# A recurrent kernel on one core: in four late steps, the order of the candidate seed and of the update gate's activations is that of the steps before them, and two steps place one filling unit elsewhere

## The chip, the cores and the metric

The kernel runs on one core of a Trainium2 chip. The metric is the device time of one execution in microseconds (us); the time of a kernel is the median of several runs. Engines are called as the profile calls them: PE (TensorE matmuls), PEld (its weight loads), DVE (VectorE), ACT (ScalarE), POOL (GpSimd), SP (SyncE, which issues most DMAs).

## What is computed

A gated recurrent unit runs over 128 steps for 64 sequences of width 512, in float32, and its outputs are added to its inputs. Every fourth step but the last passes the state through one more matrix (a "prop" step).

```python
def step(h, inp):
    x_t, prop = inp
    comb = jnp.concatenate([x_t, h], axis=-1)
    z = jax.nn.sigmoid(comb @ Wz + bz)
    r = jax.nn.sigmoid(comb @ Wr + br)
    comb2 = jnp.concatenate([x_t, r * h], axis=-1)
    h_cand = jnp.tanh(comb2 @ Wh + bh)
    h_new = (1.0 - z) * h + z * h_cand
    h_next = jnp.where(prop, jnp.tanh(h_new @ Wp + bp), h_new)
    return (h_next, h_new)
...
x = x + _L0_cond_ref(x, cond_1024, ...)     # h0 is cond_1024; prop in steps 3, 7, ... 123
```

## The kernel before

**Two halves.** The 64 sequences are split in two halves of 32, called half 0 and half 1 (`h` in the code). Each half is a Python generator, `half(h)`, that emits the instructions of its steps and yields the columns of each piece of PE work; a loop at the end always advances the half that has emitted fewer columns, half 1 starting 700 columns behind. That sets the order of the instructions in every engine's queue. A matmul of half h uses two of the four 32-column groups of the PE array, so the matmuls of both halves run beside each other, but they are issued in one order: where the first one in the queue waits, the others wait behind it.

**One step.** For each half: the gate matmuls R (line 1076), the sigmoid of r, `rh` = r·h, its transpose `rhT` (lines 1080-1082); the gate matmuls Z (line 1092); `places[0]` filling units (line 1127); the candidate's matmuls H (line 1129), which need `rhT`; the tanh `c` (line 1134); c·z, `h` = c·z - keep, and its transpose `hT` (lines 1136-1139); `places[1]` filling units (line 1149). R of the next step needs `hT`. In a prop step the gate P follows (line 1151), its tanh `hprop`, its transpose, and `places[2]` units. Below, R0, Z0, H0, P0 are the gates of half 0 and R1, Z1, H1, P1 those of half 1, with the step in brackets: R0(122).

**Filling units.** The input's share of the gates (x times the upper half of the weights) doesn't depend on the state. It is cut in units of PE work that stand in a queue; `fill(n, h)` takes the next n. The table `PLACES` (by step modulo 8) and the table `TAIL` (for the last steps, T = 128) say how many units a step places before H, after H, and after P. For the steps up to 125 the shares are computed for four steps together by a scheme with fewer multiplications (units of 192 columns); ACT, DVE and POOL combine their results into `cp`, from which each step's share `G[t]` is read. The shares of steps 126 and 127 (`wide_step`) are made straight in PSUM by `wide_unit` (four matmuls of 128 columns a half).

**Seeds.** `seed(i, t, h)` (line 439) is an ACT copy that writes a step's share of gate i from `cp` into the PSUM bank on which the gate's matmuls then add up: `rec` for R and H of each half, `rec_z` for Z of both halves. It appears in the profile as ACT COPY at L442.

**Late steps.** `late(t)` (line 834) holds for steps 121 (T - 7) and 123, 124, 125 (and the wide steps, where no seeds are made). In other steps, called body steps here, the seed of H for step t + 1 is emitted behind the tanh of step t (line 1145), or behind the prop's transpose (line 1159). In a late step it is emitted inside the step, behind the transpose of `rh` (line 1084). In a body step, half 1 emits the sigmoids of z of both halves behind its gate Z (`gate_z(slice(0, S), range(S))`, line 1115): four ACT instructions into PSUM (`rec_z`), and one DVE instruction of 256 columns for `keep` = (z - 1)·h. In a late step, half 1 emits there only those of half 0 (line 1113); those of half 1 come behind its gate H, just ahead of its tanh (line 1133); they go to a tile `z` in SBUF (line 1096), and `keep` is made by two DVE instructions of 128 columns.

Step 121 takes the last six 192-column units; behind it, POOL makes `G[124]` and `G[125]` from them (line 911). Steps 122 to 125 take units of the wide steps. Step 123 is a prop step.

Of the kernel before, what the change touches and what calls it, by code (L numbers as in the profile page):

```python
# [9 lines left out]
F32 = mybir.dt.float32  # L10
# [8 lines left out]
def kernel(  # L19
# [15 lines left out]
    B, T, D = x.shape  # L35
    H = h0.shape[1]
    P = 128
    S = 2
    V = B // S
    NQ = P // V  # L40
    J = H // NQ
# [6 lines left out]
    R, Z, H_ = range(3)  # L48
# [10 lines left out]
    one = ctx.enter_context(tc.tile_pool(name="one", bufs=1))  # L59
# [128 lines left out]
    z = rec[2][:, 1]  # L188

    def gate_ps(i, h):  # L190
        return rec[2][:, 0] if i == Z else rec[h][:, 0 if i == R else 1]
# [63 lines left out]
    def gate(i, h, lT, w):  # L255
        for k in range(K):
            products(gate_ps(i, h), h, lT[:, h, ts(k, V)], lambda c: quarters(w)[:, c, k])
            yield S * J
# [17 lines left out]
    def crossed(dst, h, i, func, ordered=True):  # L276
        for d in range(2):
            o, v = dst[ts(d, 2 * V)], gate_ps(i, h)[ts(h, 2 * V), d, :]
            if ordered:
                o, v = state_order(o), plain_order(v)  # L280
            nc.scalar.activation(o, v, func)  # L281

    def turn(dst, src):
        nc.vector.transpose(out=dst, in_=src)
# [154 lines left out]
    def seed(i, t, h):  # L439
        if t < T - WIDE:  # L440
            rows = slice(None) if i == Z else ts(h, 2 * V)
            nc.scalar.copy(  # L442
                gate_ps(i, h)[rows].rearrange("p d (c n) -> p d c n", c=C),
                G[t][rows, :, :, i, :].rearrange("p c d n -> p d c n"),
            )
# [308 lines left out]
    def pair_right(a, p1, x_, g=1):  # L754
# [6 lines left out]
    )  # L761
    HEAD = {0: (4, 6, 0), 1: (8, 6, 0), 2: (16, 12, 0), 3: (8, 6, 8), 4: (6, 8, 0)}
    TAIL = {
        T - 10: (6, 8, 0), T - 9: (1, 7, 5), T - 8: (1, 7, 0), T - 7: (0, 6, 0), T - 6: (1, 5, 0),
        T - 5: (0, 5, 3), T - 4: (1, 5, 0), T - 3: (2, 0, 0),
    }

    WIDE = 2
# [61 lines left out]
    both(8)  # L830

    state = {0: (h_init, hT)}

    def late(t):
        return t == T - 7 or t >= T - 5

    made = {}
    kept_h = {}
# [1 line left out]
    def shared(t, name, new):  # L840
        if (t, name) not in made:
            made[t, name] = new()
        return made[t, name]

    def new_two(name, t):
        return shared(t, name, lambda: two.tile([P, S, J], F32, tag=name, name=f"{name}_{t}"))

    def new_first(t):
        return shared(t, "h", lambda: one.tile([P, S, J], F32, tag=f"h{t}", name=f"h_{t}"))

    def new_turned(tag, name, t):
        return shared(t, name, lambda: new_T(tag, f"{name}_{t}"))

    def begin(t):
        u = (t - 3) % 8
        even = FIRST + 2 * ((t - 3) // 8)
        if t == 1:
            put(batch((1, 0), [(1, 1), (1, 2)]))
        elif t == 2:
            put(batch((1, 1), [(1, 10), (1, 11)]) + batch((1, 2), [(1, 8), (1, 9)]))  # L860
        elif t == 3:
            put(batches(FIRST))
        elif u == 7:
            put(batches(even + 2))
        if t == T - 10:
            put(
                batch((LAST, 0), [(LAST - 1, 4), (LAST, 1)])
                + batch((LAST, 1), [(LAST, 2), (LAST, 10)])
                + [wide_unit(T - 2, i, k) for i in (R, Z, H_) for k in range(K)]
                + [wide_bias(T - 2), crossing_unit()]  # L870
                + [wide_unit(T - 1, i, k) for i in (R, H_, Z) for k in range(K)]
                + [wide_bias(T - 1)]
            )

    def behind_r(t, duo, u):
        odd = FIRST + 2 * duo + 1
        if t == 2:
            pair_left(0, 1, 2)
            sum_inner(7, nc.gpsimd)
        elif t == 3:  # L880
            pair_right(0, 1, 10)
        if t == 4:
            sum_inner(4, nc.gpsimd)
        if u == 0 and duo >= 1 and odd - 2 < LAST:
            outer_u2(odd - 2)
# [171 lines left out]
    def half(h):  # L1057

        for t in range(T):
            g, j = divmod(t, Q4)  # L1060
            prop = j == CHUNK - 1 and t < T - 1
            last = t == T - 1
            duo, u = divmod(t - 3, 8)
            places = HEAD.get(t) or TAIL.get(t) or PLACES[u]
            if h == 0:
                begin(t)
            if t >= T - WIDE:
                yield from wide_step(t, h)
                if last:
                    return  # L1070
                if h == 1:
                    behind_step(t, duo, u, state[t + 1][0])
                continue
            h_old, hT = state[t]

            yield from gate(R, h, hT, wh[R])
            if h == 1:
                behind_r(t, duo, u)
            rh, rhT = new_two("rh", t), new_turned("rhT", "rhT", t)
            crossed(r_, h, R, AF.Sigmoid)  # L1080
            nc.vector.tensor_mul(rh[:, h, :], r_, h_old[:, h, :])  # L1081
            turn(rhT[:, h, :], rh[:, h, :])
            if late(t) or t == 0:
                seed(H_, t, h)
            if t not in (3, T - 5):
                seed(R, t + 1, h)
            if h == 1:
                join(t, duo, u, 0)

            if t == 0:  # L1090
                yield from fill(2 * K - 2, h)
            yield from gate(Z, h, hT, wh[Z])
            keep = new_two("keep", t)
            z_ = z
            if late(t):
                z_ = shared(t, "z", lambda: one.tile([P, S, J], F32, tag="o12", name=f"z_{t}"))

            def gate_z(part, halves, h_old=h_old, z_=z_, keep=keep):
                for i in halves:
                    crossed(z_[:, i, :], i, Z, AF.Sigmoid)  # L1100
                kept = keep[:, part, :], z_[:, part, :], h_old[:, part, :]
                nc.vector.scalar_tensor_tensor(  # L1102
                    out=kept[0],
                    in0=kept[1],
                    scalar=1.0,
                    in1=kept[2],
                    op0=ALU.subtract,
                    op1=ALU.mult,
                )

            if h == 1:
                if late(t):
                    gate_z(0, (0,))
                else:
                    gate_z(slice(0, S), range(S))
                join(t, duo, u, 1)
                if t == 1:
                    sum_raw34(1)
                    sum_inner(6, nc.gpsimd)
                if t == 0:  # L1120
                    join_x(1, 0)
                    join_x(1, 1)
                    sum_raw12(1)
                if t == 2:
                    for n in range(2, 4):
                        join_x(2, n)
            yield from fill(places[0], h)

            yield from gate(H_, h, rhT, wh[H_])
            h_new = new_two("h", t) if t > 1 else new_first(t)  # L1130
            cand = new_two("c", t)
            if late(t) and h == 1:
                gate_z(1, (1,))
            crossed(cand[:, h, :], h, H_, AF.Tanh)
            c = z_[:, h, :]
            nc.vector.tensor_mul(c, cand[:, h, :], c)
            hT = new_turned("hT", "hT", t)
            nc.vector.tensor_sub(h_new[:, h, :], c, keep[:, h, :])  # L1138
            turn(hT[:, h, :], h_new[:, h, :])
            if t == T - WIDE - 1:  # L1140
                made_by[t + 1, None, h] = at[h] + 820
            if prop:
                nc.scalar.copy(gate_ps(P_, h)[ts(h, 2 * V)], bias_p[ts(h, 2 * V)])
            elif not late(t + 1):
                seed(H_, t + 1, h)
            if h == 1:
                seed(Z, t + 1, 0)
            state[t + 1] = h_new, hT
            yield from fill(places[1], h)
            if prop:  # L1150
                yield from gate(P_, h, hT, wp)
                h_next = new_two("hprop", t)
                hT = new_turned("hT", "hpT", t)
                crossed(h_next[:, h, :], h, P_, AF.Tanh)
                turn(hT[:, h, :], h_next[:, h, :])
                if t in (3, T - 5):
                    seed(R, t + 1, h)
                if not late(t + 1):
                    seed(H_, t + 1, h)
                state[t + 1] = h_next, hT  # L1160
                yield from fill(places[2], h)
            if h == 1:
                behind_step(t, duo, u, h_new)
# [6 lines left out]
    while any(live):  # L1170
        h = 0 if live[0] and (not live[1] or at[0] <= at[1]) else 1
# [46 lines left out]
```

## Time and profile before

| | us |
|---|---|
| three runs | 1254.91, 1256.15, 1256.37; median 1256.15 |
| the profiled execution's own time | 1255.74 |
| its span, from the first to the last instruction of the program | 1253.6 |
| PE busy | 1246.9 (99% of the span) |
| PEld busy | 1174.0 (94%) |
| DVE, ACT, POOL busy | 806.2, 830.0, 908.8 |
| granted clock of PE | 1.0 |

The profile is one execution, 2.1 us of which lie outside the span. Times in its timelines count from the span's start. A row of the timeline view has the start, the time from the start of the first to the end of the last of some equal instructions in a row, the engine, the line, the operation, the tile written <- the tiles read, their shapes and number, and in brackets how long the engine was idle before them and whose work ended the wait. The releaser is inferred from what ended last before, and can be another.

### The profile page before, as it was taken

What the parts mean: (1) busy time and instruction counts of PE and PEld (TensorE: products, weight loads), DVE (VectorE), ACT (ScalarE), POOL (GpSimd) and SP (SyncE); (2) the same over time, 40 slices, a digit from 0 to 9 for tenths busy, and PEclk for the clock granted to TensorE, in tenths of its full rate; (3) what the DMA queues carried; (4) which work ended last, traced back from release to release, by engine and by line L of the source; (5) the groups of instructions that cost most, each with busy time, mean ns of one, the idle gap of its engine ahead of it and who ended that gap; (6) DMA issues with size and microseconds to landing.
All of it is one profiled execution on the core that took longest, in us unless ns stands there. A gap on an engine that the chain in (4) does not pass through costs nothing.

```text
span 1253.6 us, 61573 instructions
## 1 busy us (share of the span) xinstructions
PE 1246.9 (99%) x26384; PEld 1174.0 (94%) x26384; DVE 806.2 (64%) x2177; ACT 830.0 (66%) x2666; POOL 908.8 (72%) x1032
## 2 busy tenths in 40 slices
PE   9999999999999999999999999999999999999998
PEld 5899999999999999999999999999999999999987
DVE  5666666666666666666666666666666666666554
ACT  2566666766666676766666667666666666666664
POOL 4988777777876778767778677786777777777630
PEclk9999999999999999999999999999999999999999
DMA  8311212121111110221201211111111112111011
GB/s 257 83 31 42 53 37 53 36 54 39 35 53 49 41 49 24 53 53 37 54 24 49 53 41 50 36 43 47 53 38 39 49 39 53 39 52 27 12 39 35
DMA packets 112360, 61.14 MB, mean 49 GB/s; under 512 B 12844, under 2 KB 109368, under 8 KB 112088
## 3 DMA queue, kind: packets, MB, share of 16 engines
q1 hardware_dynamic: 111656, 56.90, 16.8%
q8 instruction: 208, 3.41, 1.2%
q14 instruction: 64, 0.52, 0.1%
q0 software_dynamic: 256, 0.14, 0.1%
q10 hardware_dynamic: 176, 0.16, 0.0%
HBM read 40.38 MB, written 16.78 MB: 46 GB/s over the span
## 4 chain that ended last, share of the span: by engine, by line
PE 99%; DMA 1%; SPq 0%; DVE 0%; issue 0%; ACT 0%
PE rec L246 44%; PE rec_z L246 16%; PE scratch_r L246 14%; PE scratch_q L246 11%; PE scratch_a L246 5%; PE scratch_y L246 4%; PE scratch_x L246 4%; DMA wx<-in_L_cond_Wr_dram 1%; PE scratch_a L541 0%; PE scratch_r L541 0%; PE scratch_q L541 0%; PE scratch_y L541 0%; PE scratch_x L541 0%; SPq L127 0%; SPq L141 0%
## 5 line engine op out<-in xcount | busy, mean ns | idle before, releaser
L246 PE MATMUL rec<-wh,rhT 128*32 128x256 f32 x4032 | 370.1, 379 | 0.0
L246 PE MATMUL rec<-wh,hT 128*32 128x256 f32 x3008 | 276.2, 379 | 0.0
L246 PE MATMUL rec_z<-wh,hT 128*32 128x256 f32 x3008 | 276.2, 379 | 0.0
L246 PEld LDWEIGHTS rec<-wh,rhT 128*32 128x32 f32 x4032 | 247.5, 110 | 16.7 <-ACT rec L442 0.3
L281 ACT ACTIVATE scratch_r<-rec 64x128 f32<-64x128 f32 x504 | 126.0, 250 | 129.9 <-PE rec L246 65.4
L442 ACT COPY rec<-cp 64x256 f32<-64x256 f32 x504 | 186.9, 371 | 19.4 <-DVE cp L483 0.2
L246 PEld LDWEIGHTS rec_z<-wh,hT 128*32 128x32 f32 x3008 | 190.5, 110 | 6.2
L246 PEld LDWEIGHTS rec<-wh,hT 128*32 128x32 f32 x3008 | 184.0, 110 | 11.2 <-ACT rec_z L442 0.4
L281 ACT ACTIVATE rec_z<-rec_z 64x128 f32<-64x128 f32 x488 | 122.0, 250 | 91.3 <-PE rec_z L246 79.7
L281 ACT ACTIVATE c<-rec 64x128 f32<-64x128 f32 x504 | 136.7, 271 | 61.5 <-PE rec L246 50.4
L968 POOL TENSOR_TENSOR xr<-xr,h 128x256 f32<-128x256 f32 x125 | 109.3, 874 | 85.8 <-DVE h L1138 71.9
L711 POOL TENSOR_TENSOR cp<-mb,mb 128x768 f32<-128x768 f32 x76 | 139.1, 1830 | 9.4 <-DVE mb L677 5.7
L711 POOL TENSOR_TENSOR mb<-mb,mb 128x768 f32<-128x768 f32 x58 | 106.3, 1832 | 45.8 <-DVE mb L677 45.8
L711 POOL TENSOR_TENSOR cp<-mb 128x768 f32<-128x768 f32 x46 | 84.3, 1832 | 56.8 <-ACT rec_z L442 55.4
L246 PE MATMUL scratch_r<-tw,s 128*32 128x192 f32 x928 | 120.9, 326 | 0.0
L650 ACT COPY cq<-scratch_q 128x384 f32<-128x384 f32 x212 | 102.1, 481 | 19.4 <-PE scratch_q L246 17.9
L667 DVE TENSOR_TENSOR cx<-scratch_r,cx 128x384 f32<-128x384 f32 x106 | 59.0, 557 | 84.5 <-PE scratch_r L246 69.0
L246 PE MATMUL scratch_q<-tt,s 128*32 128x192 f32 x928 | 103.6, 326 | 0.0
L1102 DVE SCALAR_TENSOR_TENSOR keep<-rec_z,h 128x256 f32<-128x256 f32 x91 | 38.6, 424 | 95.6 <-ACT rec_z L281 89.2
L673 DVE TENSOR_TENSOR mb<-scratch_q,cx 128x384 f32<-128x384 f32 x106 | 59.0, 557 | 62.5 <-ACT cq L650 62.5
L1081 DVE TENSOR_TENSOR rh<-scratch_r,h 128x128 f32<-128x128 f32 x188 | 54.8, 292 | 59.2 <-ACT scratch_r L281 59.2
L246 PE MATMUL rec<-wp,hT 128*32 128x256 f32 x992 | 91.4, 379 | 0.0
(250 smaller groups left out, 3899.9 us busy)
## 6 DMA issues: line engine op xcount, KB each, us to landing
out_dram<-xr SPq DMA_DIRECT2D x250, 64.0 KB, 1.8
xr<-in_x_dram SPq DMA_DIRECT2D x248, 64.0 KB, 2.1
xs<-in_x_dram SPq DMA_DIRECT2D x240, 64.0 KB, 2.1
wx<-in_L_cond_Wz_dram SPq DMA_DIRECT2D x2, 512.0 KB
wx<-in_L_cond_Wh_dram SPq DMA_DIRECT2D x2, 512.0 KB, 9.5
wh<-in_L_cond_Wr_dram SPq DMA_DIRECT2D x2, 512.0 KB
wh<-in_L_cond_Wz_dram SPq DMA_DIRECT2D x2, 512.0 KB, 5.5
wh<-in_L_cond_Wh_dram SPq DMA_DIRECT2D x2, 512.0 KB
```

The source lines that it names most:

```text
L246: nc.tensor.matmul(ps[part(2 * h + c)], lhsT=left, rhs=rhs(c), start=start, stop=True, skip_group_check=True,)
L281: nc.scalar.activation(o, v, func)
L442: nc.scalar.copy(gate_ps(i, h)[rows].rearrange("p d (c n) -> p d c n", c=C), G[t][rows, :, :, i, :].rearrange("p c d n -> p d c n"),)
L650: nc.scalar.copy(c[:, :nm], ps[:, :nm])
L667: nc.vector.tensor_add(T2[what][:, :nm], r_ps[:, :nm], T2[what][:, :nm])
L673: nc.vector.tensor_add(blocks(1, 1), runs(q_ps[:, :nm]), runs(T2[what][:, :nm]))
L711: nc.gpsimd.tensor_add(dst, a, b)
L968: nc.gpsimd.tensor_add(o, o, h_new.rearrange("p h (k e) -> p h e k", k=K))
L1081: nc.vector.tensor_mul(rh[:, h, :], r_, h_old[:, h, :])
L1102: nc.vector.scalar_tensor_tensor(out=kept[0], in0=kept[1], scalar=1.0, in1=kept[2], op0=ALU.subtract, op1=ALU.mult,)
```

## The change

In four steps (121, 123, 124, 125), the H seed moves from inside the step to the end of the step before; the four sigmoids of z come together behind gate Z and write `rec_z`; `keep` is one DVE instruction. The function `late` is gone. In steps 121 and 123, one unit per half moves from behind gate H to ahead of it. The number of matmuls, of weight loads, of ACT instructions and of DMAs is as before; DVE has four instructions fewer.

```diff
     TAIL = {
-        T - 10: (6, 8, 0), T - 9: (1, 7, 5), T - 8: (1, 7, 0), T - 7: (0, 6, 0), T - 6: (1, 5, 0),
-        T - 5: (0, 5, 3), T - 4: (1, 5, 0), T - 3: (2, 0, 0),
+        T - 10: (6, 8, 0), T - 9: (1, 7, 5), T - 8: (1, 7, 0), T - 7: (1, 5, 0), T - 6: (1, 5, 0),
+        T - 5: (1, 4, 3), T - 4: (1, 5, 0), T - 3: (2, 0, 0),
     }
...
-    def late(t):
-        return t == T - 7 or t >= T - 5
-
...
             turn(rhT[:, h, :], rh[:, h, :])
-            if late(t) or t == 0:
+            if t == 0:
                 seed(H_, t, h)
...
             z_ = z
-            if late(t):
-                z_ = shared(t, "z", lambda: one.tile([P, S, J], F32, tag="o12", name=f"z_{t}"))
...
             if h == 1:
-                if late(t):
-                    gate_z(0, (0,))
-                else:
-                    gate_z(slice(0, S), range(S))
+                gate_z(slice(0, S), range(S))
...
-            if late(t) and h == 1:
-                gate_z(1, (1,))
             crossed(cand[:, h, :], h, H_, AF.Tanh)
...
-            elif not late(t + 1):
+            else:
                 seed(H_, t + 1, h)
...
                 if t in (3, T - 5):
                     seed(R, t + 1, h)
-                if not late(t + 1):
-                    seed(H_, t + 1, h)
+                seed(H_, t + 1, h)
```

## The prediction

> **What bounds the kernel now.** The page first, then the span by steps, then the weight loads, ACT and DVE around the four late steps. The page names one engine for the whole span:
>
> ```profile
> PE 1246.9 (99%) x26384; PEld 1174.0 (94%) x26384; DVE 806.2 (64%) x2177; ACT 830.0 (66%) x2666; POOL 908.8 (72%) x1032
> PE 99%; DMA 1%; SPq 0%; DVE 0%; issue 0%; ACT 0%
> ```
>
> PE has the same matmuls after the change, so all that can move is the time in which PE waits, and only from the end of step 120 on. The windows below are steps 120 to 125, each from its first sigmoid of r to the next one's. Columns: busy time and instructions of PE, PEld, DVE, ACT, POOL, then clock and DMA.
>
> ```profile
> 1190.56:1198.34 7.78, 7.78 (x167) 7.38 (x163) 4.33 (x13) 4.68 (x17) 0.96 (x2) 1.00 0.29 71
> 1198.34:1206.41 8.07, 8.07 (x159) 6.19 (x155) 4.63 (x15) 6.24 (x20) 0.00 (x0) 1.00 0.25 69
> 1206.41:1213.63 7.22, 7.22 (x187) 6.79 (x183) 3.80 (x12) 4.21 (x15) 6.55 (x4) 1.00 0.01 2
> 1213.63:1224.27 10.64, 10.64 (x270) 9.82 (x266) 4.15 (x14) 7.20 (x24) 3.25 (x4) 1.00 0.07 16
> 1224.27:1232.07 7.80, 7.80 (x197) 6.84 (x192) 3.47 (x12) 5.03 (x17) 0.87 (x1) 1.00 0.23 56
> 1232.07:1239.73 7.66, 7.66 (x229) 7.03 (x224) 3.47 (x12) 3.91 (x14) 0.67 (x1) 1.00 0.01 2
> ```
>
> PE busy hides its waits here (8.07 of 8.07): the end of a matmul is modelled. Weight loads show them. Between 1198 and 1239 us only three groups of loads have idle time ahead of them:
>
> ```profile
> 1201.14 0.36 PEld L246 LDWEIGHTS rec<-wh,rhT 128*32 128x32 f32 x10 [0.30 <-ACT rec L442]
> ...
> 1203.38 0.28 PEld L246 LDWEIGHTS scratch_q<-tt,s12r 128*32 128x32 f32 x4
> 1203.59 0.17 PEld L246 LDWEIGHTS rec<-wh,hT 128*32 128x32 f32 x4
> ...
> 1205.07 0.39 PEld L246 LDWEIGHTS rec<-wh,hT 128*32 128x32 f32 x10 [0.44 <-ACT rec_z L442]
> ...
> 1220.39 0.39 PEld L246 LDWEIGHTS rec<-wp,hT 128*32 128x32 f32 x10 [0.20 <-issue]
> ```
>
> The first is H1(121), the second R1(122), the third P1(123): 0.30 + 0.44 + 0.20 = 0.94 us. **That is all there is to win.** R0(122) at 1203.59 follows its half's last unit without a gap: half 0 has no idle time there, and none to spare.
>
> ACT and DVE in step 121, which is late, then ACT and DVE in step 122, whose order is the body's:
>
> ```profile
> 1198.90 0.83 ACT L442 COPY rec<-cp 64x256 f32<-64x256 f32 x2
> 1199.75 0.54 ACT L281 ACTIVATE scratch_r<-rec 64x128 f32<-64x128 f32 x2
> 1200.31 0.77 ACT L442 COPY rec<-cp 64x256 f32<-64x256 f32 x2
> 1201.11 0.55 ACT L281 ACTIVATE z<-rec_z 64x128 f32<-64x128 f32 x2
> 1201.85 0.55 ACT L281 ACTIVATE c<-rec 64x128 f32<-64x128 f32 x2 [0.18 <-PE rec L246]
> 1203.40 0.56 ACT L281 ACTIVATE c<-rec 64x128 f32<-64x128 f32 x2
> 1204.39 0.38 ACT L442 COPY rec_z<-cp 128x256 f32<-128x256 f32 x1
> 1206.41 0.53 ACT L281 ACTIVATE scratch_r<-rec 64x128 f32<-64x128 f32 x2 [1.15 <-DVE mb L676]
> ...
> 1200.64 0.31 DVE L284 STREAM_TRANSPOSE rhT<-rh 128x128 f32<-128x128 f32 x1
> 1203.16 0.31 DVE L284 STREAM_TRANSPOSE hT<-h 128x128 f32<-128x128 f32 x1
> 1204.64 0.31 DVE L284 STREAM_TRANSPOSE hT<-h 128x128 f32<-128x128 f32 x1
> ```
>
> ```profile
> 1208.79 1.09 ACT L281 ACTIVATE rec_z<-rec_z 64x128 f32<-64x128 f32 x4 [0.48 <-PE rec_z L246]
> 1209.91 0.55 ACT L281 ACTIVATE c<-rec 64x128 f32<-64x128 f32 x2
> 1212.25 0.38 ACT L442 COPY rec_z<-cp 128x256 f32<-128x256 f32 x1 [0.74 <-DVE h L1138]
> ...
> 1211.21 0.31 DVE L284 STREAM_TRANSPOSE hT<-h 128x128 f32<-128x128 f32 x1
> ...
> 1211.64 0.14 PEld L246 LDWEIGHTS rec<-wh,hT 128*32 128x32 f32 x3
> ```
>
> A load follows the transpose it needs by 0.12 us: hT of half 0 ends at 1203.16 + 0.31 = 1203.47, R0(122) loads at 1203.59; in step 122, 1211.52 and 1211.64. The idle before 1201.14 ends 0.19 behind rhT of half 1 (1200.95), that before 1205.07 0.12 behind hT of half 1 (1204.95). So these two waits are for DVE's transposes, not for the ACT copies that the brackets name.
>
> **The change, step by step.** *The moved seeds.* Eight copies of some 0.37 us leave the sigmoid of r's neighbourhood. In step 121, the sigmoid for half 1 (1199.75) stood behind two copies of half 0 (1198.90); with one left it starts up to 0.37 earlier, rhT is done by some 1200.6 and H1 no longer waits: the 0.30 is won, for half 1 alone. At the end of steps 120, 122 and 124, ACT has idle time around the tanhs, which takes the copies; without that cover each would cost its 0.40 with the gap. Step 123's end is dealt with below.
>
> *The z sigmoids of step 121.* From the first sigmoid of z to R0's load the late order takes 1203.59 - 1201.11 = 2.48 us, the body's 1211.64 - 1208.79 = 2.85: the tanh of half 0 now stands behind four sigmoids (1.09) instead of two. The first sigmoid still starts at about 1201.1, because Z1 ends then (step 122's waits for PE likewise). So hT of half 0 comes 0.37 later. The unit moved ahead of H0 doesn't help: the PE work between Z0 and R0 is one H gate and six units in either order. R0(122), which had no spare, moves by **+0.37**.
>
> For half 1, the tanh can start behind four sigmoids, one tanh and one seed, 1201.11 + 1.11 + 0.58 + 0.40 = 1203.20 instead of 1203.40, so its hT comes 0.2 earlier: R1(122) at some 1204.87 to 1205.0 instead of 1205.07, **-0.1**. The 0.44 held half 0 too, since R0's later matmuls were queued behind it, by about 0.2; that goes. Step 121 leaves half 0 at +0.37 - 0.2 = **+0.17** and half 1 at **-0.1**.
>
> *z in PSUM.* The Z seed for the next step now waits for the `h` of half 1 (the row at 1212.25; at 1204.39 it didn't). Behind it on ACT stands the copy of the units' result, behind that DVE's sums, and for those the sigmoid of r at 1206.41 waits, on which H0(122) hangs. All that shifts by about 0.1, and R0(122) itself by more, so it is hidden; uncovered, it costs 0.1. POOL's sums behind it are wanted only in step 124's seeds, some microseconds later. `keep` is 0.42 instead of twice 0.29 on a DVE that isn't full (4.63 of 8.07): nothing. No DMA moves past another on any queue.
>
> *Step 123.*
>
> ```profile
> 1216.59 0.55 ACT L281 ACTIVATE z<-rec_z 64x128 f32<-64x128 f32 x2 [0.79 <-PE rec_z L246]
> 1217.16 0.55 ACT L281 ACTIVATE c<-rec 64x128 f32<-64x128 f32 x2
> 1218.47 0.31 DVE L284 STREAM_TRANSPOSE hT<-h 128x128 f32<-128x128 f32 x1
> 1218.99 0.15 PEld L246 LDWEIGHTS rec<-wp,hT 128*32 128x32 f32 x3
> 1221.12 0.55 ACT L281 ACTIVATE hprop<-rec 64x128 f32<-64x128 f32 x2 [1.03 <-PE rec L246]
> 1221.70 0.37 ACT L442 COPY rec<-cp 64x256 f32<-64x256 f32 x1
> 1222.38 0.56 ACT L281 ACTIVATE hprop<-rec 64x128 f32<-64x128 f32 x2 [0.31 <-PE rec L246]
> ```
>
> With four sigmoids (1.11) the tanh of half 0 starts at 1217.70, +0.54. Its hT had 1218.99 - (1218.78 + 0.12) = 0.09 to spare: P0 +0.45, less the 0.1 by which half 1's Z1 now ends earlier: **+0.35**, the +0.17 included. P1's own 0.20 goes, since its tanh no longer stands behind z, but P1 is queued behind P0: about **+0.05**. Then the first `hprop` ends some 0.25 later, at 1221.92, and two copies stand behind it instead of one: 1222.72 for the second `hprop`, against 1222.38 now. R1(124) **+0.3**.
>
> *Steps 124 and 125.*
>
> ```profile
> 1227.11 0.55 ACT L281 ACTIVATE z<-rec_z 64x128 f32<-64x128 f32 x2
> 1228.16 0.55 ACT L281 ACTIVATE c<-rec 64x128 f32<-64x128 f32 x2 [0.50 <-PE rec L246]
> 1236.40 0.55 ACT L281 ACTIVATE c<-rec 64x128 f32<-64x128 f32 x2 [0.94 <-PE rec L246]
> ```
>
> The idle time ahead of these tanhs takes the two added sigmoids (0.55): all of it in step 125, in step 124 but for some 0.3 (half 1 being 0.3 late), which the units behind H0(124), shifted themselves, cover. Without that cover: 0.3 more.
>
> **The sum.** The wide steps need both halves, so the later one counts: +0.3 us (half 0 +0.25, half 1 +0.3). Against the profiled execution, 1255.74 + 0.3 = 1256.0; that lies 0.41 under the median of the runs shown, so against the median 1256.15 + 0.3 = **1256.45**. By its bounds the sum runs from -0.94 (every wait gone, no new one) to +2.6 (the second rival).
>
> A rule for reading PE: the Trainium skill, Perfetto Trace Analysis, Identifying the Most-Contended Engine, says that matmul busy time is a poor gauge and that the summed time of LDWEIGHTS over the window is better. The trace agrees: PE busy is full in step 121, and by it nothing could be won there; loads by their count fall from 163 in 7.78 us to 155 in 8.07, 8% of the step or 0.68 us, near the 0.30 + 0.44.
>
> **Rivals.** *All waits go and nothing replaces them:* -0.94, 1255.2. For it: three waits with known causes, each of which the change removes. Against: R0(122) has no spare for the 0.37.
>
> *The new chain decides everywhere (slower):* four sigmoids, tanh, hT, next gate. Each late step pays the 0.55 of the added sigmoids, the in-order queue hands it to both halves, and the prop pays one seed: 4 × 0.55 + 0.40 = +2.6, 1258.75. It decides where the work behind H0 ends less than 2.85 us after the first sigmoid of z. Against: 0.50 and 0.94 of idle in steps 124 and 125. If only steps 121 and 123 pay on both halves: 0.37 + 0.45 + 0.34 = +1.2, 1257.3.
>
> *The change is empty in time:* the seeds fall into idle time, the units change places, gains and losses cancel: 1256.15.
>
> *The loads come back to step 120's share.* PEld is busy 95% there (7.38 of 7.78). At that share, steps 121 to 125 would be shorter by 1.5, 0.1, 0.3, 0.6 and 0.2: -2.6, 1253.5. Against: only 0.94 has an idle group of loads beside it; elsewhere the loads of both halves coincide (ten in 0.39 us) and count once.
>
> **How the numbers follow.** The forecast has 0.35; all waits gone 0.20; slower by about 1.2, 0.18; slower by about 2.6, 0.12; empty 0.13; the loads' share 0.02. The range goes from 1255.0 (the first rival less the scatter of the runs shown) to 1258.2, which leaves out most of the +2.6 and of the -2.6; the forecast's own is 1255.6 to 1257.2. A difference of 0.2%, 2.5 us, is about what can be told from none: faster by more 0.02, within it 0.88, slower by more 0.10.
>
> **What would show it.** H1(121) without idle loads: the seeds' step is right. In step 121, two pairs of sigmoids in one group of 1.09 and a tanh right behind it, then an idle group at R0(122) of some 0.3 to 0.4, and none at R1(122): the order's step. Idle loads at P0(123) instead of P1(123), and a second `hprop` right behind two copies: step 123. No idle loads in 124 and 125. Wrong: R0(122) without idle time (then it is the first rival), or idle loads before R0(125) and the first wide gate (the second).

## The result and the profile after

| | before | after |
|---|---|---|
| median of 22 runs each, us | 1255.58 (1254.52 to 1256.81) | 1257.06 (1255.98 to 1259.12) |
| ratio after / before, 95% interval | | 1.0014 (1.0007 to 1.002) |
| the profiled execution, us | 1255.74 | 1257.27 |
| its span, us | 1253.6 | 1255.2 |

The change makes the kernel slower by 0.14%, some 1.5 us. The forecast was 0.3 us slower, 1256.45; the side was right and the size was not. The time itself lies only 0.6 above 1256.45, and part of that nearness is luck: the median of three runs on which the forecast stood lies 0.57 above that of 22. The difference is within the 0.2% that the prediction took as the bound of what can be told, but 22 runs tell it.

Of the 1.6 us between the two spans, 0.46 lies ahead of anything that changed: the first sigmoid of r of step 120 starts at 1190.56 before and at 1191.02 after, and the order of the instructions is the same up to the end of step 120. In e1 to e9 below, which leave everything ahead of that end alone, this start lies between 1189.79 and 1191.52, so it says nothing of the change. From it to the first sigmoid of the wide steps, the stretch in which all that changed lies, it is 49.17 us before and 50.29 after: **+1.12 us**. This stretch (windows view, one window over all six steps) is used below, since stretches of this kind repeat well: steps 118 and 119, which are the same in the two kernels and in e1 to e9, take 20.85 or 20.86 us in every one of them, while single runs scatter by a microsecond.

The windows view of the changed kernel, step by step, 120 to 125, with the columns of the prediction's:

```profile
1191.02:1198.80 7.78, 7.78 (x167) 7.42 (x163) 4.37 (x13) 5.42 (x19) 0.96 (x2) 1.00 0.32 80
1198.80:1206.90 8.10, 7.88 (x160) 7.09 (x156) 4.48 (x14) 5.42 (x18) 0.00 (x0) 1.00 0.22 60
1206.90:1214.18 7.28, 7.28 (x190) 7.04 (x185) 3.77 (x12) 4.95 (x17) 6.60 (x4) 1.00 0.01 2
1214.18:1225.73 11.55, 11.42 (x270) 9.03 (x266) 4.00 (x13) 7.12 (x25) 3.21 (x4) 1.00 0.13 30
1225.73:1233.56 7.83, 7.83 (x199) 6.63 (x195) 3.43 (x11) 4.95 (x18) 0.87 (x1) 1.00 0.13 31
1233.56:1241.31 7.75, 7.75 (x228) 7.41 (x224) 3.42 (x11) 3.08 (x12) 0.88 (x1) 1.00 0.01 3
```

Against 8.07, 7.22, 10.64, 7.80 and 7.66 before, step 123 carries 0.91 of the 1.12. Step 121 is as long as before, though its waits are others. The groups of weight loads with idle time ahead of them (timeline of PEld, the whole stretch):

```profile
1204.40 0.14 PEld L246 LDWEIGHTS rec<-wh,hT 128*32 128x32 f32 x3 [0.57 <-ACT c L281]
...
1216.10 0.14 PEld L541 LDWEIGHTS scratch_r<-wx,xT 128*32 128x32 f32 x3 [0.58 <-DVE rh L1078]
...
1220.24 0.14 PEld L246 LDWEIGHTS rec<-wp,hT 128*32 128x32 f32 x3 [0.27 <-ACT c L281]
...
1223.63 0.11 PEld L246 LDWEIGHTS rec<-wh,hpT 128*32 128x32 f32 x2 [0.25 <-ACT rec L442]
...
1225.02 0.36 PEld L246 LDWEIGHTS rec<-wh,hpT 128*32 128x32 f32 x10 [0.38 <-ACT rec L442]
```

They are R0(122), the filling unit ahead of H0(123), P0(123), R0(124) and R1(124). The three old waits are gone, as forecast, and five new ones sum to 2.05 us against 0.94. That this is 1.11 more, nearly the 1.12 of the stretch, is a coincidence: in step 121 the waits fall by 0.17 and the step is 0.03 longer, in step 123 they rise by 1.28 and it is 0.91 longer, and 0.18 stands in steps 122, 124 and 125, where no wait is named. So the waits show where PE stood, and the stretch what it cost. Two of the five were forecast in their place and kind (R0(122), P0(123)), one in its place and size but not wholly in its cause (R1(124)), two not at all.

The one at 1216.10 has a clear releaser. DVE and ACT of the changed kernel there:

```profile
1215.75 0.29 DVE L1078 TENSOR_TENSOR rh<-scratch_r,h 128x128 f32<-128x128 f32 x1 [0.37 <-ACT scratch_r L281]
...
1222.81 0.31 DVE L284 STREAM_TRANSPOSE hpT<-hprop 128x128 f32<-128x128 f32 x1 [1.77 <-ACT hprop L281]
1224.19 0.31 DVE L284 STREAM_TRANSPOSE hpT<-hprop 128x128 f32<-128x128 f32 x1 [1.07 <-ACT hprop L281]
```

```profile
1215.18 0.53 ACT L281 ACTIVATE scratch_r<-rec 64x128 f32<-64x128 f32 x2 [0.47 <-PE rec L246]
...
1218.50 0.55 ACT L281 ACTIVATE c<-rec 64x128 f32<-64x128 f32 x2 [0.17 <-PE rec L246]
...
1222.23 0.55 ACT L281 ACTIVATE hprop<-rec 64x128 f32<-64x128 f32 x2 [1.07 <-PE rec L246]
1222.81 0.77 ACT L442 COPY rec<-cp 64x256 f32<-64x256 f32 x2
1223.60 0.56 ACT L281 ACTIVATE hprop<-rec 64x128 f32<-64x128 f32 x2
1224.19 0.77 ACT L442 COPY rec<-cp 64x256 f32<-64x256 f32 x2
```

DVE's r·h of half 1 ends at 1216.04, and the unit's loads start at 1216.10. That r·h reads `scratch_r`, for the sigmoid of r has its 128 columns in that bank (`r_ = scratch[r_bank][:, 3 * J :]`, line 198), and the unit that step 123 now places ahead of H0 writes other columns of the same bank. Likewise at the end of the prop: the two copies behind the first `hprop`, the seeds of R and H, end at 1223.58, and R0(124) loads at 1223.63; the two behind the second end at 1224.96, and R1(124) loads at 1225.02. The transposes that these loads need end at 1223.12 and 1224.50, half a microsecond earlier, so they are not what the loads wait for. R0 doesn't read the H seed, but both lie in one tile, `rec`, of one bank a half (line 187).

### The profile page after: what moved, and what is told of

It reads as the page before. It is cut to its first block, busy times and chain, and to the rows that moved or that the text cites. A ratio compares the mean times of both kernels' runs of the same rounds, so it can differ in the third digit from the quotient of the medians.

```text
span 1255.2 us, 61559 instructions
## 1 busy us (share of the span) xinstructions
PE 1248.3 (99%) x26384; PEld 1170.8 (93%) x26384; DVE 806.2 (64%) x2173; ACT 829.7 (66%) x2666; POOL 909.1 (72%) x1032
## 4 chain that ended last, share of the span: by engine, by line
PE 99%; DMA 1%; ACT 0%; SPq 0%; DVE 0%; issue 0%; DVEq 0%
PE rec L246 44%; PE rec_z L246 16%; PE scratch_r L246 14%; PE scratch_q L246 10%; PE scratch_a L246 5%; PE scratch_y L246 4%; PE scratch_x L246 4%; DMA wx<-in_L_cond_Wr_dram 1%; PE scratch_a L541 0%; PE scratch_r L541 0%; PE scratch_q L541 0%; PE scratch_y L541 0%; PE scratch_x L541 0%; SPq L127 0%; ACT rec_z L281 0%
## 5 line engine op out<-in xcount | busy, mean ns | idle before, releaser
L281 ACT ACTIVATE rec_z<-rec_z 64x128 f32<-64x128 f32 x504 | 126.0, 250 | 95.9 <-PE rec_z L246 83.9
L246 PE MATMUL rec<-wh,hpT 128*32 128x256 f32 x992 | 91.4, 379 | 0.0
```

The costliest lines, as they stand in the source:

```text
L246: nc.tensor.matmul(ps[part(2 * h + c)], lhsT=left, rhs=rhs(c), start=start, stop=True, skip_group_check=True,)
```

## The experiments

The theory after the result: the program's waits go by PSUM banks, and two parts of the change put PE work behind a bank that ACT or DVE still uses: the unit of step 123 (`scratch_r`) and the H seeds of step 124 (`rec`). The rest, four sigmoids ahead of the tanh, shifts a wait from half 1 to half 0 and is even. In this kernel each such bank is one tile of the program, so no run here can tell a wait by bank from a wait by tile. Rivals: the late R1(123) is the cause, or the moved units delay H0 and with it the tanh, or the z order costs by itself.

| | edit | stretch, us | median, ratio to before (95%) |
|---|---|---|---|
| before | | 49.17 | |
| after | all of the change | 50.29 | 1257.06, 1.0014 (1.0007 to 1.002) |
| e1 | after, step 123's unit back | 49.82 | 1256.34, 1.0005 (0.9996 to 1.0014) |
| e2 | after, step 121's unit back | 50.29 | 1256.70, 1.0009 (1.0000 to 1.0018) |
| e3 | after, sigmoid of r of step 123 in SBUF | 49.87 | 1256.61, 1.0003 (0.9994 to 1.0012) |
| e4 | after, late z order in step 121 | 50.71 | 1257.08, 1.0012 (1.0003 to 1.0021) |
| e5 | before, early seeds alone | 49.66 | 1256.18, 1.0005 (0.9996 to 1.0014) |
| e6 | before, units' places alone | 50.47 | 1257.05, 1.0011 (1.0002 to 1.0020) |
| e7 | before, z order alone | 49.16 | 1255.82, 0.9999 (0.9990 to 1.0008) |
| e8 | before, z by each half | 52.62 | 1260.01, 1.0031 (1.0019 to 1.0042) |
| e9 | e1, step 124's H seeds back | 49.12 | 1255.55, 1.0001 (0.9993 to 1.0010) |

The medians of the kernel before beside these lay between 1255.57 and 1255.76. Experiments e10 and e11 change steps 118 and 119 too and stand further below.

**e1: step 123's unit back behind H.**

```diff
-        T - 5: (1, 4, 3), T - 4: (1, 5, 0), T - 3: (2, 0, 0),
+        T - 5: (0, 5, 3), T - 4: (1, 5, 0), T - 3: (2, 0, 0),
```

> The changed kernel with step 123's unit back behind gate H (0, 5, 3); all else as changed. Theory (the unit waits because it writes scratch_r, the PSUM bank in which the sigmoid of r stands until rh is made): the idle 0.58 us ahead of a scratch_r load at step 123 is gone; P0(123) still waits for the chain of four sigmoids (some 0.2 to 0.6 us idle, more than the 0.27 of the changed kernel, as part of the 0.58 had covered it). Sum of idle weight-load time in steps 121 to 125 falls from 2.05 us to 1.5 to 1.7, time 0.3 to 0.6 below the changed kernel. Rival (the wait is for the late R1(123) itself): an idle group of about the same length shows at H0(123) instead.

The wait for r·h is gone; the view of waits has no row for it, and the three in the timeline of PEld of e1 are

```profile
1204.68 0.14 PEld L246 LDWEIGHTS rec<-wh,hT 128*32 128x32 f32 x3 [0.56 <-ACT c L281]
...
1223.44 0.11 PEld L246 LDWEIGHTS rec<-wh,hpT 128*32 128x32 f32 x2 [0.26 <-ACT rec L442]
...
1224.83 0.36 PEld L246 LDWEIGHTS rec<-wh,hpT 128*32 128x32 f32 x10 [0.38 <-ACT rec L442]
```

The stretch falls by 50.29 - 49.82 = 0.47 us. P0(123), expected to wait at least as long as the changed kernel's 0.27, is no longer among the waits that the timeline names: without the unit, H0 and its tanh come earlier. In the changed kernel that tanh waited 0.17 us for H0 (the row at 1218.50); in e1 it follows the four sigmoids at once. What the sigmoids do to P0 is left: it loads 28.74 us behind the start of step 120 in e1, against 28.43 before.

**e3: the unit stays, the sigmoid of r of step 123 goes to SBUF.**

```diff
-            crossed(r_, h, R, AF.Sigmoid)
-            nc.vector.tensor_mul(rh[:, h, :], r_, h_old[:, h, :])
+            r_t = r_
+            if t == T - 5:
+                r_t = shared(t, "r", lambda: one.tile([P, S, J], F32, tag="o12", name=f"r_{t}"))[:, 0]
+            crossed(r_t, h, R, AF.Sigmoid)
+            nc.vector.tensor_mul(rh[:, h, :], r_t, h_old[:, h, :])
```

> The changed kernel with one thing different: in step 123 alone, the sigmoid of r goes to an SBUF tile instead of scratch_r. Theory (bank shared by the filling unit and the sigmoid of r): the 0.58 us idle ahead of the scratch_r load is gone though the unit is still ahead of H0; P0(123) waits longer than 0.27, up to 0.6. Rival (the unit waits for something else, such as its turn behind half 1): the 0.58 stays.

The same unit, at the same place in PE's order, now loads without idle time, and earlier by 0.64: 24.44 us behind the start of step 120 (1215.11 - 1190.67) instead of 25.08 (1216.10 - 1191.02). The timeline of PEld of e3:

```profile
1215.11 0.36 PEld L541 LDWEIGHTS scratch_r<-wx,xT 128*32 128x32 f32 x4
```

The stretch is 49.87, 0.42 less than with the shared bank. That shows the cause: neither the unit's turn nor R1(123), but the bank. One part of the expectation fell: P0(123) has no named wait here either, instead of one longer than 0.27.

**e2 and e4: step 121's unit back; or the late z order in step 121.** e2 has `T - 7: (0, 6, 0)`; e4 has, in step 121 alone,

```diff
+            if t == T - 7:
+                z_ = shared(t, "z", lambda: one.tile([P, S, J], F32, tag="o12", name=f"z_{t}"))
...
-                gate_z(slice(0, S), range(S))
+                if t == T - 7:
+                    gate_z(0, (0,))
+                else:
+                    gate_z(slice(0, S), range(S))
...
+            if t == T - 7 and h == 1:
+                gate_z(1, (1,))
```

> The changed kernel with step 121's unit back behind gate H (0, 6, 0); all else as changed. Theory (R0(122) hangs on the chain: first sigmoid of z, four sigmoids, tanh, hT; where the unit stands is neutral for it): R0(122) idle stays at 0.5 to 0.6 us, H1(121) has no idle group since the H seeds are out of the way. Time within 0.2 us of the changed kernel. Rival (the moved unit delays H0 and so the tanh): R0(122) idle falls by about a unit, 0.3 us.

> The changed kernel with the late order of the z sigmoids (half 1's behind gate H, in SBUF) in step 121 alone; seeds and units as changed. Theory (the added pair of sigmoids ahead of the tanh of half 0 is what R0(122) waits for): the idle 0.57 us at R0(122) falls by 0.25 to 0.4, limited by H0, which stands one unit (0.33 us) later; some idle comes back at R1(122). Rival (R0(122) waits because H0 is later by a unit): it stays above 0.5.

In e2, R0(122) waits 0.56 instead of 0.57, and the stretch is the same (the median is 0.36 below the changed kernel's, which the intervals don't tell from none): with four sigmoids ahead of the tanh, the unit's place is neutral, as the prediction argued. In e4, the wait at R0(122) falls only to 0.48, and 0.46 comes back at R1(122); the stretch grows by 0.42 (timeline of PEld of e4):

```profile
1203.32 0.14 PEld L246 LDWEIGHTS rec<-wh,hT 128*32 128x32 f32 x3 [0.48 <-ACT z L281]
1204.82 0.39 PEld L246 LDWEIGHTS rec<-wh,hT 128*32 128x32 f32 x10 [0.46 <-ACT rec_z L442]
```

So the expectation fell: the wait is 0.09 shorter, not 0.25 to 0.4. The rival's bound, above 0.5, is just missed too, but its mechanism is the one seen: with the late order, the unit ahead of H0 does hold up the tanh. Two chains of nearly one length lead to R0(122), through the sigmoids and through H0; taking one away leaves the other. In e5 below, which has neither, the wait is 0.20.

**e5, e6, e7: each part of the change alone.** e5 drops `late` from the three conditions on the H seed, e6 takes the new entries of `TAIL`, e7 takes the body's z order.

> The kernel before with the early H seeds alone (z order and units as before). From the first sigmoid of r of step 120 to that of the first wide step, the kernel before takes 49.18 us and the changed one 50.30. Theory (the chain to hT decides, not the seeds): the 0.30 idle at H1(121) goes, but the tanh of half 1 still stands behind its z sigmoids, so the idle at R1(122) grows from 0.44 to 0.5 to 0.7, and nothing is won in step 121; behind step 123's prop the second seed delays the second hprop: 0.2 to 0.4 of idle at R1(124). Stretch 49.2 to 49.6. Rival (the seeds were the cause of the waits): stretch 48.6 to 48.9.

> The kernel before with the units' places alone (0,6,0 to 1,5,0 in step 121 and 0,5,3 to 1,4,3 in step 123). Theory: in step 123 the unit ahead of H0 writes the bank of the sigmoid of r and waits 0.5 to 0.6 us for half 1's rh; in step 121 the unit delays H0, and with it the tanh and R0(122), by up to 0.33. Stretch (49.18 before) 49.8 to 50.1, most of the loss of the change. Rival (units neutral, the z order costs): within 0.2 of 49.18.

> The kernel before with the z order alone (four sigmoids behind gate Z, in PSUM; seeds and units as before). Theory: R0(122) waits 0.5 to 0.6, the waits at R1(122) and P1(123) of 0.44 and 0.20 go or move to half 0, no wait at R1(124) as large as 0.38, since only one seed stands behind the prop. Stretch (49.18 before) 49.2 to 49.6. Rival (the z order is the main cost): 49.9 or more.

The z order alone is even: 49.16 against 49.17. In e7 the waits at R1(122) and P1(123) are gone; H1(121) keeps its 0.30, and R0(122) waits 0.31, less than the 0.5 to 0.6 expected. The seeds alone cost 0.49, a little above the range expected: the wait at H1(121) goes, but 0.20 comes at R0(122) and R1(122) keeps 0.41 instead of growing; the rest is step 123, 0.34 longer, and steps 124 and 125, 0.19 longer together. At the end of step 123's prop the view of waits of e5 has, for PE's loads behind the copies,

```profile
PEld rec L246 <- ACT rec L442: 0.4, 1, 0.4
```

The units alone cost 1.30 (50.47, where 50.1 at most was expected): with the late order the moved unit delays the tanhs in both steps (timeline of PEld of e6):

```profile
1203.09 0.14 PEld L246 LDWEIGHTS rec<-wh,hT 128*32 128x32 f32 x3 [0.48 <-ACT z L281]
1204.58 0.39 PEld L246 LDWEIGHTS rec<-wh,hT 128*32 128x32 f32 x10 [0.46 <-ACT rec_z L442]
...
1215.28 0.14 PEld L541 LDWEIGHTS scratch_r<-wx,xT 128*32 128x32 f32 x3 [0.57 <-DVE rh L1081]
...
1219.42 0.14 PEld L246 LDWEIGHTS rec<-wp,hT 128*32 128x32 f32 x3 [0.27 <-ACT z L281]
1220.91 0.39 PEld L246 LDWEIGHTS rec<-wp,hT 128*32 128x32 f32 x10 [0.46 <-issue]
```

The parts don't add up: -0.01 + 0.49 + 1.30 = 1.78, and together they cost 1.12. The z order and the early seeds take away part of what the units cost.

**e9: e1, with step 124's H seeds back inside step 124.**

```diff
-            if t == 0:
+            if t in (0, T - 4):
                 seed(H_, t, h)
...
-                seed(H_, t + 1, h)
+                if t != T - 5:
+                    seed(H_, t + 1, h)
```

> The changed kernel with step 123's unit back behind H (as in e1) and, besides, step 124's H seeds back inside step 124, so that one copy instead of two stands behind each hprop. Theory (the second copy between the two hprops holds back half 1): the idle of 0.38 at R1(124) that e1 shows goes to at most 0.1, and the stretch from step 120 to the first wide step falls from e1's 49.82 by 0.2 to 0.4, to 49.4 to 49.6. Rival (R1(124) is late because of the z order in step 123): 0.38 and 49.8 stay.

The stretch falls by 49.82 - 49.12 = 0.70, more than expected: both waits at step 124, 0.26 and 0.38, are gone. In the timeline of PEld of e9 one wait is left in the whole stretch:

```profile
1204.89 0.14 PEld L246 LDWEIGHTS rec<-wh,hT 128*32 128x32 f32 x3 [0.57 <-ACT c L281]
```

With the 0.47 of e1, step 123's unit and step 124's early seeds make 1.17 of the change's 1.12; all else in it is worth -0.05. The 0.70 has two parts that e9 takes away together: the second `hprop` starts 31.76 us behind the start of step 120 instead of e1's 32.11, as the theory of the queue on ACT has it, and R1(124) no longer waits the 0.38 for the copies behind that `hprop`.

**e8: each half's z behind its own gate Z.** A try to do better than both: no tanh would stand behind the other half's z.

```diff
-            if late(t) or t == 0:
+            if t in (0, T - 4):
                 seed(H_, t, h)
...
-            if h == 1:
-                if late(t):
-                    gate_z(0, (0,))
-                else:
+            if late(t):
+                gate_z(h, (h,))
+            if h == 1:
+                if not late(t):
                     gate_z(slice(0, S), range(S))
...
-            if late(t) and h == 1:
-                gate_z(1, (1,))
...
-            elif not late(t + 1):
+            else:
                 seed(H_, t + 1, h)
...
-                if not late(t + 1):
+                if t != T - 5:
                     seed(H_, t + 1, h)
```

> The kernel before with the z sigmoids of each half emitted behind that half's own gate Z in the late steps (so neither tanh stands behind the other half's z), and early H seeds except for step 124, whose seed stays inside the step. Theory (what decides is what stands ahead of each tanh on ACT): the idle groups at H1(121), R1(122) and P1(123), 0.94 us, fall to at most 0.3; stretch 48.4 to 48.8 against 49.18, time 0.4 to 0.8 us below the kernel before. Rival (half 0's z waits for half 1's gate Z anyway, or a new wait appears at R0): stretch 49.0 or more.

It is 3.45 us slower in the stretch, where 0.4 to 0.8 faster was expected. Its view of waits has one row for PE's loads:

```profile
PEld rec_z L246 <- ACT z L281: 4.2, 4, 1.5
```

Z1's matmuls, which write the bank `rec_z` while half 0's z is read from it, now wait in each late step for that read. The halves use different partitions of the bank; the wait is there all the same.

**e10 and e11: more work behind H0(121).** Both have the change's z order and the H seed of step 124 inside the step. e10 is built on the kernel before, with the early H seed in step 121 alone, and moves two units from step 118 to step 121; e11 is e9 with one unit from behind step 119's prop. Of their edits, the table:

```diff
 e10
-        T - 10: (6, 8, 0), T - 9: (1, 7, 5), T - 8: (1, 7, 0), T - 7: (0, 6, 0), T - 6: (1, 5, 0),
+        T - 10: (4, 8, 0), T - 9: (1, 7, 5), T - 8: (1, 7, 0), T - 7: (1, 7, 0), T - 6: (1, 5, 0),
 e11
-        T - 10: (6, 8, 0), T - 9: (1, 7, 5), T - 8: (1, 7, 0), T - 7: (1, 5, 0), T - 6: (1, 5, 0),
+        T - 10: (6, 8, 0), T - 9: (1, 7, 4), T - 8: (1, 7, 0), T - 7: (1, 6, 0), T - 6: (1, 5, 0),
```

> A version meant to beat both: the z order of the change in all steps, the early H seed in step 121 alone, step 123's units as before, and two units moved from step 118 (6,8,0 to 4,8,0; it has fourteen) to step 121 (1,7,0 like step 120). Theory (R0(122) waits because six units are too little cover for the chain through four sigmoids; eight are enough, as in step 120): no idle loads at H1(121), R0(122) or R1(122), at most 0.2 left in step 123. From the first sigmoid of r of step 118 to that of the first wide step: 70.03 before, 71.15 changed; 69.2 to 69.6 here. Time 0.4 to 0.9 below the kernel before. Rival (the units are missed in step 118, or POOL's sums come too late): 70.0 or more.

> The kernel of e9 with one unit moved from behind step 119's prop (1,7,5 to 1,7,4) to behind gate H of step 121 (1,5,0 to 1,6,0). Theory (R0(122) waits for the chain through four sigmoids because the work behind H0(121) is about one and a half units too little; and a filling unit costs a wait only where it writes scratch_r ahead of H): idle at R0(122) falls from 0.57 to 0.2 to 0.3, no other idle group above 0.2 appears in steps 119 to 125. From the first sigmoid of r of step 118 to that of the first wide step: 70.03 before, 71.15 changed, 69.98 in e9; 69.6 to 69.8 here. Time 0.2 to 0.4 below the kernel before, too little to be told from it by the runs. Rival (the shift by one unit brings a scratch_r unit or a bank still being read ahead of H somewhere, as in e10): an idle group of 0.5 or more, 70.3 or more.

e10: 1258.74, ratio 1.0022 (1.0013 to 1.0031), and 72.43 us from step 118 on, where 69.2 to 69.6 was expected. Behind R0(121), which waits 0.30, no wait is named up to the wide steps, as its theory said. But shifted by two, the queue puts a `scratch_r` unit ahead of H0(119), and the same wait is there, longer (timeline of PEld of e10):

```profile
1182.18 0.11 PEld L246 LDWEIGHTS scratch_r<-tw,s4r 128*32 128x32 f32 x2 [1.11 <-DVE rh L1081]
1187.60 0.14 PEld L246 LDWEIGHTS scratch_r<-tw,s4r 128*32 128x32 f32 x3 [1.92 <-issue]
```

The second, 1.92, has no releaser in PEld's row; PE's row for the matmul behind it has one (timelines of PE and DVE of e10):

```profile
1187.63 0.36 PE L246 MATMUL scratch_r<-tw,s4r 128*32 128x192 f32 x2 [1.58 <-DVE cx L667]
...
1186.96 0.52 DVE L667 TENSOR_TENSOR cx<-scratch_r,cx 128x384 f32<-128x384 f32 x1
```

DVE's read of the units' last result in `scratch_r` ends at 1187.48, and the unit loads at 1187.60. DVE had that read behind the two halves' chains to `hT`. No experiment was made on this second wait.

e11: 1255.40 against 1255.54, ratio 0.9997 (0.9988 to 1.0006). Its wait at R0(122) is 0.24:

```profile
1203.07 0.14 PEld L246 LDWEIGHTS rec<-wh,hT 128*32 128x32 f32 x3 [0.24 <-ACT c L281]
```

From step 118 to the wide steps, the window rows are, before and in e11,

```profile
1169.71:1239.73 70.02, 70.02 (x1620) 63.99 (x1616) 35.95 (x111) 45.29 (x151) 23.92 (x19) 1.00 0.10 26
```

```profile
1169.17:1238.82 69.65, 69.65 (x1620) 65.91 (x1616) 35.63 (x107) 44.98 (x152) 24.09 (x19) 1.00 0.10 26
```

0.37 us less than before and 1.50 less than the changed kernel's 71.15, with the same number of matmuls. That e11 beats the kernel before is seen in these stretches alone; the runs can't tell it.

## Why the prediction was right on the side and wrong in the size

*The bound.* PE's waits in steps 121 to 125 were all that could move, and weight loads with idle time ahead of them showed where it stood. Their sum is no measure of the time: in e1 it is 0.26 above the kernel before and the stretch 0.65, in e9 0.37 below and the stretch 0.05. PEld's busy time isn't one either: step 121 has 6.19 of 8.07 before and 7.09 of 8.10 after. Why a wait costs more or less than its length was not tested.

*What the first wait is for.* The prediction read the waits at 1201.14 and 1205.07 as waits for transposes alone, "not for the ACT copies that the brackets name". For the second that fits the 0.12 us of other loads behind their transposes. The first ends 0.19 behind its transpose, but 0.06 behind the two copies that end at 1201.08, as the loads at 1216.10, 1223.63 and 1225.02 come 0.05 to 0.06 behind the last use of their bank. The copies cost H1(121) little there, for the transpose would have let it load 0.07 earlier; but the second of them, the seed of R(122), is nothing that H1(121) reads, so PE waiting for a copy into its bank stood in the kernel before already.

*The moved seeds.* Right for step 121 (H1 no longer waits). Right also, as far as named waits show it, that three of the four step ends hide the copies.

*The z sigmoids of step 121.* Right: R0(122) became the wait (0.57, where 0.37 and no spare were forecast), the waits at H1(121) and R1(122) went, and the step as a whole stayed even, 8.10 against 8.07. e7 shows the z order to be even over all four steps.

*The units' places.* **This is the step that failed**: "The unit moved ahead of H0 doesn't help: the PE work between Z0 and R0 is one H gate and six units in either order." That holds in step 121 (e2). For step 123 the same was taken without a look at which bank the moved unit writes. It writes the bank of the sigmoid of r: 0.58 of wait, 0.47 of the stretch (e1), and 0.42 us won back when only the sigmoid moved (e3). The sum had no term for it.

*The end of step 123.* The mechanism was half right: the second `hprop` stands behind two copies. The term was 0.3, and the early seeds of step 124 measured 0.70 (e9), because R0(124) and R1(124) also wait for the second copy itself, which writes their bank. The copy was costed as an occupant of ACT's queue only, and as such it was costed well: from the start of step 120, the second `hprop` starts 0.29 later in e1 than before, where 0.34 was forecast. This term, mis-sized by 0.4, is nearly as much of the miss as the unit.

*P0(123) and steps 124, 125.* The +0.35 at P0 was right: from the start of step 120, P0 loads 0.31 later than before in e1 and 0.35 later in e7, which have the four sigmoids and not the moved unit. That the changed kernel shows a wait of 0.27 there is partly something else, the H0 that the unit held up. Behind the loads of R0(124) and R1(124), steps 124 and 125 showed no idle group, as said.

*The rivals.* The slower one (1.2 if only steps 121 and 123 pay) came near the measured time by luck, for the mechanism that it named is not the one that cost: not the chain through four sigmoids, which e7 shows to be even, but banks.

A page states the rule that both misses come under. The Trainium skill, PSUM — Partial Sum Buffer, PSUM bank collisions raise a hardware error, has it that engines must be kept apart by bank and quadrant of partitions, not by address. The waits at 1216.10 and 1223.63 agree for different columns of one bank; e8's wait is between different partitions of one bank, where the rule by quadrant would need none, so this program's waits are wider than that rule.

## What to carry to other kernels

In a program like this one, before PE work is moved earlier, look up the PSUM bank that it writes and who else uses that bank at the new place; other columns don't help, and the order in which filling work stands in a queue is matched to the banks (e10 shows what a shift by two does). A seed copied into a bank is a wait for all PE work on that bank, also for what doesn't read it, so it belongs where that bank is idle. With two chains of like length to one gate, an experiment that removes one of them shows little; remove each, and both (e2, e4, e5). And read a change's cost from a stretch that holds all of it, not from the sum of the waits.

## What was not expected of the hardware

PE's matmul rows were full in every step before the change (8.07 of 8.07) with waits of 0.30 and 0.44 inside, and nearly so after it (7.88 of 8.10 with a wait of 0.57). Its loads came 0.12 us behind a transpose that they needed, and 0.05 to 0.06 behind the last use of their bank by ACT or DVE, which told the two kinds of wait apart where the brackets did not. One load of e10 came 0.12 behind a DVE read of its bank, so the distance alone is no proof. And the start of step 120 differs by up to 1.7 us between executions of the same instructions (1189.79 to 1191.52), more than the whole effect of the change.
